# Row statistics taken chunk by chunk, later rotation tables on GpSimd, column statistics by pairs, zero fill behind the loads: one change to a fused decoder kernel

## The chip, the cores and the metric

The kernel runs on one core of a Trainium2 chip. The metric is device time in microseconds for one execution of the whole program; the median of three runs before the change is 1200.24 us (1200.2 to 1203.42). The profile is of one further execution.

## The reference, cut to what matters

Input `x` has 8 sequences of 256 rows and 1024 features, so 2048 rows. Three branches are added to it one after the other, each on a layer norm (without weights) of what came before.

```python
x = x + attn(_layernorm(x), ...)            # 4-layer decoder, width 128, on the sequences
x = x + xattn(_layernorm(x), ctx_4096, ...) # channel mask from the context, gates, conv, batch norm
x = x + ffn(_layernorm(x), gate_w, expert_w)# 8 experts of 1024x1024, two for each row

# attn: h = LN(x) @ Win.T + bin, then four times:
y = silu(layernorm(h, l1w, l1b))
y = sconv(y, phazor, last_conv)  # causal convolution with p**t, p = tanh|phz| * exp(i*angle)
h = h + y * scl
y = silu(layernorm(h, l2w, l2b) @ w1.T + b1) @ w2.T + b2
h = h + y
# and: layernorm(h) @ Wout.T + bout
# xattn: for each (sequence, feature) column the top 154 of 256 rows of ctx are "kept":
_, topk_idx = jax.lax.top_k(cm, k)
mask = zeros.at[b_idx, l_idx, topk_idx].set(1.0)
kept, dropped = mask * LN(x), (1 - mask) * LN(x)  # max and mean of both give two gates
```

## The kernel before, in words

**Tiling.** Features lie on the 128 partitions. The 2048 rows are four chunks of 512 (two sequences each); `xs[c]` holds chunk c as 128 partitions x 8 feature groups x 512. All arithmetic is fp32.

**Row statistics.** The projection needs mean and standard deviation of each row of `x`. For these, `x` is loaded a second time with rows on the partitions: `load_rows(c)` (L380) brings 2 MB into a tile of the pool `maskp` (tag `mask`, one buffer, the later home of the mask), takes `bn_stats` of 4 x 2 stretches of 512 on VectorE (L387), `bn_aggr` (L388), and a power of -1/2 on GpSimd (L393). L396 to L407 issue the loads on SyncE's queue: rows and x of chunk 0, the first quarter of the context, `w1`, `w2`, then rows and x of chunks 1, 2, 3 with a second quarter of the context between. Behind them L408 to L413 queue a zero fill of 9 MB (18 DMAs of 512 KB) into the output and one block of a scratch tensor.

**Tables.** Layer l's convolution is written as: multiply by cos and sin of the phase, a real scan with `decay`, multiply again. The table `turn` (4 layers x cos and sin x 256) is doubled in eight steps by angle addition in `phases(some)` (L426): for layer 0 alone four VectorE instructions a step (L439 to L442), for layers 1 to 3 together six (L446 to L451). L453 starts a block of high priority, in which the powers of the phase, the table of layer 0 (L495), `decay`, the initial values and `turned_w` are traced. After it come the centring of `win` (L517 to L530), `start(0)`, two steps of search, and the folding of `w1`, `w2`, `b1`, `b2` (L548 to L565).

**Cells.** Each of 16 cells (layer, chunk) goes through `recurrence` (L583: `inverse_std` of h, y, silu, table, four scans L594, table L597), `second_norm` (L600) and `feedforward` (L614). `inverse_std` (L568) is a chain over four engines: square on ScalarE, eight small matmuls L574, `ve` on VectorE L351, the power on GpSimd L352, four broadcasting transposes L166. `start(c)` (L532) projects chunk c into h[c]. The loop L687 runs recurrence of cell n, then second_norm of n-1, feedforward of n-2, and for the last layer `put_out` and `normed_x1` of n-3 and `kept_and_dropped` of n-4 (L306: for each column of the chunk kept and dropped values, their max on VectorE L315 and sums on ScalarE L318). The tables of layers 1 to 3 are traced at n = 0 (L691), `weights_out` (load and folding of `wout`) at n = 4.

**Search.** Beside this a threshold search over the context finds the mask. Each of four quarters (16 columns by 128 partitions) is a generator (`search`, L204): a guess from `bn_stats` of each column (L216), four trials of 16 ScalarE activations that count (L233), a finish on VectorE (three instructions a column, L255 to L258), and the mask (L281). `advance(n)` (L289) traces n of these sections; two searches can be under way, the second from the third step on. Context tiles have tag `ctx` and two buffers. One detail of L216 matters: `bn_stats` gives count, mean and squared deviation of the even-numbered elements in fields 0 to 2 and of the odd ones in 3 to 5, and the guess reads fields 1 and 2 alone.

**Order.** The code is traced once. A scheduler then orders each engine's instructions, by the order of tracing as priority and by when its own model of times says an input is ready; every engine then runs its list strictly in that order. A tile with one buffer can be loaded again only when its last reader is done.

**Afterwards** come the gates and convolution, the routing, and a long stage in which TensorE multiplies rows by expert weights.

Of the kernel before, what the change touches and what calls it, by code (L numbers as in the profile page):

```python
# [9 lines left out]
F32 = mybir.dt.float32  # L10
U8 = mybir.dt.uint8
# [5 lines left out]
P = 128  # L17
# [50 lines left out]
def decoder_kernel(ctx: ExitStack, tc: tile.TileContext, x_t, x_rows, ctx_t, vecs, win_t, w1_t, w2_t, wout_t,  # L68
# [106 lines left out]
    with ExitStack() as early:  # L175
# [28 lines left out]
        def search(hb):  # L204
# [10 lines left out]
            for i in range(GH):  # L215
                v.bn_stats(st[:, i, :], ctx_h[:, i, :])  # L216

            sd = small("sd")
            v.tensor_scalar(sd, st[:, :, 2], 2.0 / S, TINY, ALU.mult, ALU.add)
# [4 lines left out]
            v.scalar_tensor_tensor(trial[:, 0], sd, -SHARE, st[:, :, 1], ALU.mult, ALU.subtract)  # L224
# [64 lines left out]
        def advance(n):  # L289
            nonlocal steps  # L290
            for _ in range(n):
                if waiting and (not going or (len(going) == 1 and steps >= 3)):
                    going.append(waiting.pop(0))
# [34 lines left out]
        with ExitStack() as dec:  # L328
# [50 lines left out]
            rows = []  # L379
            def load_rows(c):  # L380
                r = maskp.tile([P, CT // P, D], F32, tag="mask", name="rows")
                nc.sync.dma_start(out=r, in_=x_rows[c])
                mv = lp.tile([P, 4, 2], F32, tag="mv", name="mv")
# [13 lines left out]
            load_x(0)  # L397
            ctxs.append(load_ctx(0))
            nc.sync.dma_start(out=w1, in_=w1_t)
            nc.sync.dma_start(out=w2, in_=w2_t)  # L400
            load_rows(1)
            load_x(1)
            load_rows(2)
            load_x(2)
            ctxs.append(load_ctx(1))
            load_rows(3)
            load_x(3)  # L407

            zero = tkp.tile([P, S], F32, tag="hid", name="zero")
            nc.gpsimd.memset(zero, 0.0)  # L410
            for rows_ in [x2_rows[0:P, :]] + [out[i * P : (i + 1) * P, :] for i in range(NT + 1)]:
                nc.sync.dma_start(out=rows_.rearrange("p (a w) -> p a w", w=S),
                                  in_=zero.unsqueeze(1).to_broadcast([P, D // S, S]))  # L413


            mask = maskp.tile([P, B, NK, S], U8, tag="mask", name="mask")


            v = nc.vector
# [5 lines left out]

            def phases(some):  # L426

                one = some.stop - some.start == 1
                cos, sin = turn[:, some, 0, :], turn[:, some, 1, :]
                v.memset(cos[:, :, 0:1], 1.0)  # L430
                v.memset(sin[:, :, 0:1], 0.0)
                for m, (pc, ps) in enumerate(powers):
                    n = 1 << m
                    lo, hi = slice(0, n), slice(n, 2 * n)
                    tmp = lp.tile([P, 2, 2, S], F32, tag="mi", name="tab_tmp")
                    tmp = tmp.rearrange("p a b t -> p (a b) t")[:, 0 : some.stop - some.start, lo]
# [16 lines left out]
            with tc.high_priority():  # L453
# [57 lines left out]
                for l in range(DEPTH):  # L511
                    v.tensor_scalar(turned_w[:, l], center, col("sc_lin", l), None, ALU.mult)
# [768 lines left out]
```

## Time and profile before

| what | value |
|---|---|
| median of three runs | 1200.24 us |
| profiled execution | 1200.54 us, span 1198.8 us |
| TensorE busy (matmul records) | 1000.2 us, 83% of the span |
| VectorE busy | 580.4 us, 48% |
| ScalarE busy | 476.4 us, 40% |
| GpSimd busy | 261.9 us, 22% |
| mean granted TensorE clock | 0.90 |
| DMA | 144.99 MB, mean 121 GB/s |

How to read it: shares over the whole span hide that stages have different limits, so the stages are read one by one. In the rows of the timeline the first number is the start in us from the start of the span, the second the duration in us, then engine, line, operation and tiles, and in brackets the idle time of the engine before it with what ended it. In the rows by stage each engine has busy us and, in brackets, its number of instructions; then come the granted clock, the DMA share and GB/s.

### The profile page before, as it was taken

To read this page: it belongs to the slowest core of one execution; us is meant where nothing else is said; L and a number is where in the kernel's file an instruction comes from. 1 tells how busy PE (TensorE), PEld (TensorE's weight loads), DVE (VectorE), ACT (ScalarE), POOL (GpSimd) and SP (SyncE) were. 2 spreads that over 40 slices of the span, in tenths; PEclk is the share of its full clock that TensorE was granted. 3 is DMA by queue.
4 is the path that set the end of the run, shared out by engine and by line. 5 is a ranking of instruction groups with operands and counts; after the bars stand their busy time and mean duration, and the time that the engine had idled before them with its cause. 6 is when DMAs were issued, how large, how long until landed. Compare 5 with 4: busy or idle time off the path is not lost. (4 is left out here: it accounts for less than half of the span.)

```text
span 1198.8 us, 10179 instructions
## 1 busy us (share of the span) xinstructions
PE 1000.2 (83%) x2954; PEld 493.5 (41%) x2954; DVE 580.4 (48%) x1779; ACT 476.4 (40%) x1167; POOL 261.9 (22%) x275
## 2 busy tenths in 40 slices
PE   4848878878888666268649999999999999999994
PEld 2524434434444333134324444444444444444442
DVE  7588888868958988687635111111111111111110
ACT  0577667676773566595211121111111111111110
POOL 1111111121111000104367321112313214131111
PEclk9768889889989877577669999999999999999998
DMA  9495010000000000035534956463648567583622
GB/s 386 190 384 165 0 71 1 36 36 1 1 1 1 0 1 1 12 141 194 158 107 127 329 149 169 110 171 84 197 113 240 138 193 213 133 247 91 175 35 37
DMA packets 53840, 144.99 MB, mean 121 GB/s; under 512 B 5232, under 2 KB 14448, under 8 KB 51984
## 3 DMA queue, kind: packets, MB, share of 16 engines
q0 software_dynamic: 17728, 59.88, 20.3%
q1 hardware_dynamic: 35472, 83.97, 19.9%
q8 instruction: 25, 0.41, 0.1%
q10 hardware_dynamic: 576, 0.41, 0.1%
q14 instruction: 39, 0.32, 0.1%
HBM read 106.61 MB, written 37.64 MB: 120 GB/s over the span
## 5 line engine op out<-in xcount | busy, mean ns | idle before, releaser
L1091 PE MATMUL ps_mm<-w_x,xT 128*128 128x512 f32 x1152 | 505.4, 597 | 3.2 <-ACT xT L1085 1.0
L1091 PEld LDWEIGHTS ps_mm<-w_x,xT 128*128 128x128 f32 x1152 | 216.4, 190 | 270.8 <-issue 258.9
L1094 DVE SCALAR_TENSOR_TENSOR y<-ps_mm,held,y 128x512 f32<-128x512 f32 x56 | 42.0, 751 | 358.9 <-PE ps_mm L1091 358.9
L233 ACT ACTIVATE tkj<-ctx,tk_trial 128x256 f32<-128x256 f32 x256 | 129.1, 504 | 40.1 <-DVE tk_trial L248 22.7
L1077 ACT ACTIVATE y<-src,held 128x1024 f32<-128x1024 f32 x28 | 32.1, 1147 | 188.2 <-DMA out_dram<-y,to 155.1
L1085 ACT COPY xT<-ps_tp 128x512 f32<-128x512 f32 x37 | 21.6, 585 | 193.6 <-PE ps_tp L1083 181.4
L352 POOL TENSOR_TENSOR rs<-ve,minus_half 128x4 f32<-128x4 f32 x36 | 41.1, 1141 | 246.7 <-DVE ve L351 224.2
L618 PE MATMUL ps_tp<-z,w 128*128 128x512 f32 x128 | 70.6, 658 | 13.8 <-DVE z L611 12.9
L1095 POOL DMA_INDIRECT out_dram<-y,to x28 | 44.4, 1586 | 162.5 <-DVE y L1094 120.6
L166 PE MATMUL ps_st<-ident,rs 128*128 128x128 f32 x160 | 30.0, 323 | 56.3 <-POOL rs L352 48.0
L1064 POOL DMA_INDIRECT src<-x_rows,to x28 | 29.0, 1036 | 162.0 <-ACT y L1077 160.8
L318 ACT ACTIVATE comb<-comb 128x256 f32<-128x256 f32 x128 | 51.5, 403 | 27.2 <-DVE smax L315 25.5
L624 PE MATMUL ps_mm<-f,w 128*128 128x512 f32 x128 | 62.0, 604 | 0.0
L1094 DVE SCALAR_TENSOR_TENSOR y<-ps_mm,got,y 128x512 f32<-128x512 f32 x18 | 13.5, 750 | 99.8 <-PE ps_mm L1091 93.1
L166 PEld LDWEIGHTS ps_st<-ident,rs 128*128 128x128 f32 x160 | 20.8, 161 | 82.0 <-POOL rs L352 71.9
L621 ACT ACTIVATE f<-ps_tp,b1f 128x512 f32<-128x512 f32 x64 | 43.5, 681 | 24.2 <-PE ps_tp L618 23.8
L1083 PE MATMUL ps_tp<-ident,xn 128*128 128x128 f32 x296 | 39.9, 278 | 13.9 <-ACT xn L1075 13.9
L1083 PEld LDWEIGHTS ps_tp<-ident,xn 128*128 128x128 f32 x296 | 35.4, 144 | 33.4 <-issue 19.0
L574 PEld LDWEIGHTS ps_cols<-mean_w,sq 128*128 128x128 f32 x288 | 38.9, 199 | 23.2 <-ACT sq L571 11.6
L233 ACT ACTIVATION_READ_ACCUMULATOR tkj<-ctx,tk_trial 128x1 f32 x256 | 48.3, 189 | 0.0
L604 PE MATMUL ps_mm<-mi,turned_w 128*128 128x512 f32 x64 | 38.2, 704 | 7.9 <-DVE mi L597 7.8
L964 POOL DMA_INDIRECT meta<-pay,at x32 | 36.0, 1124 | 39.3 <-DVE ts_mv L889 18.9
(370 smaller groups left out, 1441.8 us busy)
## 6 DMA issues: line engine op xcount, KB each, us to landing
w_x<-in_expert_w_dram SPq DMA_DIRECT2D x36, 1024.0 KB, 7.5
out_dram<-zero SPq DMA_DIRECT2D x17, 512.0 KB, 7.3
rows<-in_x_rows_dram SPq DMA_DIRECT2D x4, 2048.0 KB, 8.3
x<-in_x_t_dram SPq DMA_DIRECT2D x8, 1024.0 KB, 11.5
ctx<-in_ctx_t_dram SPq DMA_DIRECT2D x16, 512.0 KB, 8.3
x_rows<-row SPq DMA_DIRECT2D x16, 512.0 KB, 4.9
w<-in_w_t_dram SPq DMA_DIRECT2D x2, 1024.0 KB, 10.6
win<-in_win_t_dram SPq DMA_DIRECT2D x1, 512.0 KB, 3.9
```

The costliest lines, as they stand in the source:

```text
L166: nc.tensor.transpose(rb[:, q * P : (q + 1) * P], rs[:, q : q + 1].to_broadcast([P, P]), ident)
L233: nc.scalar.activation(junk, ctx_h[:, i, :], AF.Sign, bias=trial[:, 0, i : i + 1], accum_out=trial[:, 1, i : i + 1])
L318: nc.scalar.activation(comb[:, st, :], comb[:, st, :], AF.Copy, accum_out=ssum[:, st, b, k : k + 1])
L352: nc.gpsimd.tensor_tensor(out_, ve, root, ALU.pow)
L574: nc.tensor.matmul(out=st[:, q : q + 1], lhsT=sq[:, q * P : (q + 1) * P], rhs=mean_w, start=True, stop=True)
L618: nc.tensor.matmul(out=fps, lhsT=w1[:, l, f * P : (f + 1) * P], rhs=z, start=True, stop=True)
L621: nc.scalar.activation(ft, fps, AF.Silu, bias=b1[:, 4 * l + f : 4 * l + f + 1])
L624: nc.tensor.matmul(out=xc, lhsT=w2[:, l, f, :], rhs=ft, start=False, stop=(f == DFF // P - 1), skip_group_check=True)
L1083: nc.tensor.transpose(tp[:, k * P : (k + 1) * P], xn[:, kk * P : (kk + 1) * P], ident)
L1091: nc.tensor.matmul(out=op, lhsT=xT[:, k * P : (k + 1) * P], rhs=ws[k][g], start=(k == 0), stop=(k == NK - 1))
L1094: nc.vector.scalar_tensor_tensor(y[:, o], op, weight, y[:, o], ALU.mult, ALU.add)
L1095: added = nc.gpsimd.indirect_dma_start(out=out[0:ROWS_THEN, :] if apart else out, out_offset=bass.IndirectOffsetOnAxis(ap=token, axis=0), ...
```

## The change

Four things are edited, and a few that go with them.

1. `load_rows` only loads; the statistics are a function of their own, `rows_std(c)`. Chunk 0's is traced behind the loads, that of chunk n+1 in the loop, ahead of `start(n+1)`. Row tiles of odd chunks use a buffer of tag `ctx` instead of `mask`. The loads are in a new order: rows and x of chunks 0 and 1, context quarter 0, `w1`, `w2`, x of 2 and 3, rows of 2; rows of 3 are loaded at n = 0 and context quarter 1 at n = 2.
2. `phases` becomes a generator that runs on VectorE for layer 0 and on GpSimd for layers 1 to 3; of the latter, three doubling steps are traced at each of n = 1, 2, 3, the first instruction of each step behind `y` of the current cell (`begun`). Its temporary is of tag `sq`.
3. The search's guess takes one `bn_stats` for two columns: it reads 128 even-numbered elements of each, interleaved, so that fields 0 to 2 are those of the first column and 3 to 5 those of the second.
4. The zero fill is traced at n = 4, behind `y` of cell 4 and the load of `wout`; its source is a tile of tag `sq` of 1024 elements.

Beside these: the centring of `win` moves ahead of the tables, the table of layer 0 and `turned_w` leave the high-priority block, the folding of `w1` and `w2` moves to n = 1, that of `wout` to n = 8. `advance` gets one step at n = 0 and 1 (three before), and a second search starts from the fourth step.

```diff
-            for i in range(GH):
-                v.bn_stats(st[:, i, :], ctx_h[:, i, :])
+            for i in range(0, GH, 2):
+                v.bn_stats(st[:, i : i + 2, :].rearrange("p c f -> p (c f)")[:, 0:6],
+                           ctx_h[:, i : i + 2, ::2].rearrange("p c s -> p s c"))
...
-                if waiting and (not going or (len(going) == 1 and steps >= 3)):
+                if waiting and (not going or (len(going) == 1 and steps >= 4)):
...
             def load_rows(c):
-                r = maskp.tile([P, CT // P, D], F32, tag="mask", name="rows")
+                if c % 2:
+                    r = tkp.tile([P, CT // P, D], F32, tag="ctx", name="rows", bufs=2)
+                else:
+                    r = maskp.tile([P, CT // P, D], F32, tag="mask", name="rows")
                 nc.sync.dma_start(out=r, in_=x_rows[c])
+                loaded.append(r)
+
+            def rows_std(c):
+                r = loaded[c]
                 mv = lp.tile([P, 4, 2], F32, tag="mv", name="mv")
...
             load_rows(0)
             load_x(0)
+            load_rows(1)
+            load_x(1)
             ctxs.append(load_ctx(0))
             nc.sync.dma_start(out=w1, in_=w1_t)
             nc.sync.dma_start(out=w2, in_=w2_t)
-            load_rows(1)
-            load_x(1)
+            load_x(2)
+            load_x(3)
+            rows_std(0)
             load_rows(2)
-            load_x(2)
-            ctxs.append(load_ctx(1))
-            load_rows(3)
-            load_x(3)
...
                 one = some.stop - some.start == 1
+                v = nc.vector if one else nc.gpsimd
...
+                    behind = list(begun)
-                    v.tensor_tensor(cos[:, :, hi], cos[:, :, lo], cb, ALU.mult)
+                    after(v.tensor_tensor(cos[:, :, hi], cos[:, :, lo], cb, ALU.mult).ins, behind, "in turn")
...
+            start(0)
+            advance(2)
+            table = phases(slice(1, DEPTH))
             for n in range(len(cells) + 4):
                 if n < len(cells):
                     scanned[n] = recurrence(*cells[n])
-                if n == 0:
-                    phases(slice(1, DEPTH))
                 if n + 1 < NCH:
+                    rows_std(n + 1)
                     start(n + 1)
+                    if n == 0:
+                        load_rows(3)
+                    if n == 1:
+                        weights_in()
+                    if n == 2:
+                        ctxs.append(load_ctx(1))
+                    if n == 1:
+                        mask = maskp.tile([P, B, NK, S], U8, tag="mask", name="mask")
+                if 0 < n < NCH:
+                    for _ in itertools.islice(table, 3):
+                        pass
                 if n == NCH:
-                    wo, wo_mean, bo_mean = weights_out()
+                    wo = load_wo()
+                    zeroes()
+                if n == NCH + 4:
+                    wo_mean, bo_mean = weights_out(wo)
...
-                advance(3)
+                advance(1 if n < 2 else 3)
```

`weights_in()` holds the folding of `w1` and `w2` as it was; `zeroes()` holds the zero fill.

## The prediction

> **What bounds the kernel now.** The page's chain of work that ended last only says that TensorE ends the run (it covers 1% of the span), so I read the busy times by stage first. Columns: TensorE, weight load, VectorE (DVE), ScalarE (ACT), GpSimd (POOL), clock, DMA.
>
> ```profile
> 0.00:41.00 41.00, 20.28 (x67) 14.52 (x67) 29.31 (x150) 8.95 (x25) 7.93 (x36) 0.92 0.86 347
> 41.00:82.00 41.00, 25.23 (x57) 12.81 (x57) 29.66 (x101) 25.37 (x82) 7.16 (x5) 0.71 0.74 280
> 82.00:410.00 328.00, 274.79 (x905) 139.96 (x904) 269.49 (x811) 223.20 (x614) 46.58 (x41) 0.91 0.11 38
> 410.00:490.00 80.00, 45.34 (x138) 24.37 (x138) 66.49 (x259) 54.33 (x227) 5.89 (x13) 0.71 0.00 1
> 490.00:640.00 150.00, 94.12 (x339) 50.31 (x340) 103.15 (x340) 63.64 (x114) 54.87 (x65) 0.69 0.40 123
> 640.00:1198.80 558.80, 540.44 (x1453) 251.50 (x1451) 82.26 (x120) 100.95 (x106) 139.46 (x115) 0.99 0.58 158
> ```
>
> From 640 us on TensorE is busy at clock 0.99 with expert rows: the change doesn't touch that, nor 490 to 640 (gates, routing). What the change can move is the stretch to 490. There no engine is full; VectorE is the fullest: 336.0 of the 408 us from 82 to 490, that is 82%, with 72 us idle. TensorE has 84% of 82 to 410 but only 57% after that. Before 82 VectorE is busy 59.0 of 82. So I look at the order of its work there (timeline of VectorE):
>
> ```profile
> 52.87 0.17 DVE L248 TENSOR_TENSOR tk_trial<-tk_ends,tk_w 128x16 f32<-128x16 f32 x1
> 59.39 1.88 DVE L387 BATCH_NORM_STATS2 bn<-rows 128x6 f32<-128x512 f32 x3 [6.34 <-DMA rows<-in_x_rows_dram]
> ...
> 72.40 1.88 DVE L387 BATCH_NORM_STATS2 bn<-rows 128x6 f32<-128x512 f32 x3 [1.49 <-DMA rows<-in_x_rows_dram]
> ...
> 77.94 0.16 DVE L351 TENSOR_SCALAR ve<-ps_cols 128x4 f32<-128x4 f32 x1
> ...
> 81.30 0.69 DVE L586 TENSOR_TENSOR y<-h,ps_st 128x512 f32<-128x512 f32 x1 [1.80 <-PE ps_st L166]
> ```
>
> and what TensorE (its timeline) and the load queue do:
>
> ```profile
> 44.08 1.71 PE L574 MATMUL ps_cols<-mean_w,sq 128*128 128x1 f32 x8
> 45.65 13.44 PE L536 MATMUL ps_tp<-x,win 128*128 128x512 f32 x24
> ```
> ```profile
> 51.04 0.33 SPq L382 DMA_DIRECT2D rows<-in_x_rows_dram  x1
> ```
> ```profile
> 64.48 0.33 SPq L382 DMA_DIRECT2D rows<-in_x_rows_dram  x1
> ```
>
> The first cell's variance (L574) is done at 45.8, but VectorE takes it up (L351) at 77.94, because the statistics of rows 1, 2 and 3 stand ahead of it in its list, and rows 2 and 3 can each be loaded (51.04, 64.48) only after the one buffer was read. The first cell's `mi` (L591) starts at 82.9, some 40 us later than its inputs would allow, and VectorE idles 23 us before 82.
>
> **The parts, with their cost.** *Statistics by chunk, loads, weight folding.* Nothing is removed: eight `bn_stats` and what goes with them took 45.96 to 51.57, so 5.6 us a chunk. What moves is their place: behind cell n's recurrence. Then cell 0 depends on win, x0, rows 0. h[0] came out of VectorE (L541) at 34.0, after waiting for a GpSimd power that ended at 33.65 (2.8 us of idle), and TensorE then ran the folding of `w1` (L561, 35.4 to 42.4) ahead of L574; that folding now sits at n = 1. From h at 33: bias and square on ScalarE 1.3, L574 1.1 to 1.7, `ve` 0.2, power 1.0, L166 1.1 to 2.0, y 0.7, table load and silu 1.3 + 0.8: `mi` at about 41 instead of 82.9. By then VectorE has done what it did by 41 before (29.3), less the reduction of `w2` (L549, 2.3) and half of one quarter's `bn_stats` (2.7), plus rows_std(1), whose rows now have their own buffer (5.6): 30. The new order on SyncE's queue (rows 2 behind rows_std(0), then rows 3, context 1) costs nothing while the data come before use: the 14 MB moved in the first 41 us (347 GB/s) cover win, rows and x 0 and 1, context 0, `w1`, `w2`, part of x2. x3 and rows 2 end near 50, rows_std(2) is due near 60. Without that cover it costs what it did: 6.3 us a chunk.
>
> *Tables on GpSimd.* VectorE loses L446 to L451: six lines of 2.0 to 2.07 us, 12.1 us. GpSimd gets 48 `tensor_tensor` with 4590 elements in all. The nearest row is its `tensor_tensor` L754, 129 elements in 0.525 us; its 8-element cast takes 0.18, so I take 0.17 us + 2.75 ns an element: 8.2 + 12.6 = 21 us, in blocks of 3.4, 5.8 and 11.6 us at n = 1, 2, 3. Behind them in GpSimd's list wait the powers of `inverse_std`, and behind these TensorE's L166. In the cell stage two powers lie 6 to 8 us apart, so only the third block overhangs, by some 4 us. I charge 3 us; bounds 0 (VectorE and TensorE have other cells' work) and 10 (every block delays one power by half).
>
> A rule speaks against this part. VectorE and GpSimd meet in this trace:
>
> ```profile
> 259.60 1.23 DVE L597 TENSOR_TENSOR mi<-mi,turn 128x1024 f32<-128x1024 f32 x1
> ```
> ```profile
> 259.78 1.91 POOL L352 TENSOR_TENSOR rs<-ve,minus_half 128x4 f32<-128x4 f32 x1 [6.92 <-DVE ve L351]
> ```
> ```profile
> 493.89 0.52 POOL L754 TENSOR_TENSOR vacant<-vacant,past 128x129 f32<-128x129 f32 x1
> 493.92 0.58 DVE L806 TENSOR_SCALAR zc<-row,vec 128x128 f32<-128x128 f32 x1
> ```
>
> The power takes 1.01 us alone and 1.91 when it comes behind L597. The other way round, VectorE's L808 has a median of 0.352 and took 0.506 beside an L754: 0.15 us on a GpSimd instruction of 0.53, or 30%. The Trainium skill (SBUF — State Buffer, Who interferes with whom) says more: a VectorE instruction with two SBUF inputs and a GpSimd one that reads SBUF block each other for a whole instruction. Scans, L591, L597 and L257 are of that kind, 100 of the 253 us from 82 to 335, 40%. By the row: 21 x 0.4 x 0.3 = 2.5, I take 3 us. By the rule: nearly the remaining GpSimd time whenever one of them is next, 21 x 0.4 to 0.5, or 8 to 10 us; then the move gives back most of its 12.1. I keep 10 as the bound.
>
> *Column statistics by pairs.* 64 instructions at a pitch of 0.336 us become 32 of as many elements: 10.8 us less, half before 82 and half in the cells. The new read jumps to another column at every element. The skill (the same page, Specifications) wants two hits per 16-byte line for full rate; at half rate one takes near 0.6, and only 2.3 us are saved. The nearest row: L224 reads 16 elements 24 bytes apart in 0.179 us, its neighbours L225 and L226 without that 0.175 and 0.168. No row here strides wider, so I take the nearest, 10.8, and keep 2.3.
>
> *Zero fill, `wout`, `advance`.* The fill occupied SyncE from 65.9 to 97.6; nothing on VectorE waited for it, and behind it stands a context load that waits for its buffer to 163.9. At n = 4 (near 120 to 150) it stands ahead of the same load: 0. If the buffer is free earlier, that load is up to 30 us late, which search's slack takes. The folding of `wout` moves within the cells: 0.
>
> **Sum.** VectorE to 490: 395.0 - 12.1 - 10.8 + 3 = 375. Of this 30 is done by 41; 345 remain. I keep the share of 82 to 490 (0.8235), since the same chains and orders make its idle time: 419, end at 460 instead of 490. With 3 us for the table's blocks: 27 us less, 1200.54 - 27 = 1173.5 in the profiled execution. That ran 0.3 us above the median of 1200.24: 1173.
>
> **Rivals.**
> - *Cells keep their pace* (16.7 us from L591 to L591), so the whole advance of 41 us survives: 1159. For: VectorE's load shrinks. Against: cells 0 to 3 now hold the statistics.
> - *The costs go to their bounds*: stride at half rate, blocking 10: 390.5 - 32 = 358.5, / 0.8235 = 435, end 476, with 8 us of table delays 484: 1194.
> - *The change doesn't do what it says*: the planner still puts statistics of rows 2 and 3 ahead of the first `ve`, because its model lets rows land early. Then `mi` waits for rows 3 (near 60) and some 12 us of idle remain: 1185.
> - *Slower: the search becomes the end.* Context 1 takes the rows' buffer, so it is loaded after rows_std(3) (near 87), lands near 97, and its first trial ends near 125 instead of 114.9. Eleven more trials at the old 22.5 us give 372, the last mask 51 us later, 423 (412.8 before). `kept_and_dropped` of chunk 3 began at 474.8, now 447: slack 24. It decides once trials are over 2.2 us longer; at 28 us (ScalarE shared with denser cells) the end is 36 us beyond the slack: 1173 + 36 = 1209. Against: ScalarE is only 68% busy there.
>
> **Chances and range.** Main 0.58 (own range 1162 to 1184), pace kept 0.13, bounds 0.12, planner 0.09, search 0.08. The range 1157 to 1193 leaves out the search, and parts of the pace and bounds cases. 0.3% (3.6 us) is about what a measurement tells from no change: faster 0.89, within 0.03, slower 0.08.
>
> **What would show it.** Right: first L591 near 41; no wait of L387 for rows over 2 us; L446 to L451 on GpSimd at about 21 us; 32 L216 at 0.34; the last L315 near 460; 490 to 1199 shifted as a block. Wrong: L216 near 0.6; scans and L597 stretched beside GpSimd; the cell stage's VectorE share below 0.8; L315 of chunk 3 waiting for the mask.

## The result, and the profile after

The changed kernel takes 1211.91 us (median of four runs, 1210.1 to 1213.42), the kernel before on the same chip 1201.22: a ratio of 1.0086, 95% interval 1.0064 to 1.0107. It is 0.9% slower; 1173 was forecast. The profiled execution of the changed kernel took 1213.42 us, span 1211.7, against 1200.54 and 1198.8.

Four events cut the stretch that the change touches: the first `mi` (L610, L591 before), the fifth, the sixteenth and last, and the end of the column sums of `kept_and_dropped` (L321, L315 before). Each is taken at the start of the instruction, the last one for a group. First the changed kernel by these stages, with the rest as the last row; columns as in the prediction's first view.

```profile
0.00:40.60 40.60, 21.60 (x65) 12.24 (x66) 32.22 (x147) 5.52 (x7) 8.04 (x39) 0.87 0.96 394
40.60:133.60 93.00, 70.14 (x223) 38.66 (x223) 55.18 (x123) 51.73 (x151) 40.98 (x59) 0.80 0.21 83
133.60:309.70 176.10, 152.88 (x534) 79.67 (x533) 139.84 (x406) 126.46 (x347) 33.12 (x28) 0.95 0.21 81
309.70:499.60 189.90, 119.65 (x347) 59.88 (x345) 153.63 (x563) 120.42 (x437) 12.07 (x19) 0.77 0.00 1
499.60:1211.70 712.10, 634.93 (x1790) 301.51 (x1790) 185.53 (x461) 166.03 (x228) 195.14 (x180) 0.92 0.54 150
```

and the kernel before:

```profile
0.00:82.90 82.90, 45.63 (x122) 27.34 (x122) 59.00 (x252) 35.20 (x108) 15.09 (x41) 0.81 0.80 315
82.90:148.30 65.40, 54.07 (x185) 29.43 (x186) 56.15 (x174) 48.75 (x139) 7.53 (x9) 0.87 0.35 117
148.30:333.60 185.30, 154.73 (x511) 77.95 (x511) 152.02 (x457) 131.15 (x362) 31.86 (x26) 0.91 0.06 23
333.60:487.40 153.80, 111.20 (x349) 56.95 (x347) 127.33 (x438) 95.01 (x333) 13.08 (x19) 0.84 0.00 1
```

The rest is a block: 712.1 us against 711.4. So all of the loss is in the end of the sums, 499.6 instead of 487.4. The first `mi` did come 42.3 us earlier. At the fifth 14.7 of these are left, at the sixteenth 23.9, and at the end it is 12.2 us late. The numbers to read are VectorE's (the third engine of each row): up to the fifth `mi` it did 87.4 us of work instead of 115.2, and after it 293.5 instead of 279.4, although it has 13.6 us less to do in all (380.9 against 394.5). So behind the fifth `mi` there are 14 us more work and 13 us more idle time (72.5 against 59.7), and these are more than the 14.7 us that it came earlier. The loss itself lies behind the last `mi`: from there to the end it is 189.9 us instead of 153.8, and most of the difference stands ahead of the last cell's output `h` (101.4 us to it instead of 72.0, with 74.1 us of VectorE work instead of 56.9). TensorE's work is no larger: 364.3 us up to the end, 365.6 before.

Where the first cells lost their lead stands in the timelines of the changed kernel, first TensorE's, then VectorE's, and behind them VectorE's row for the same `z` in the kernel before. (ScalarE had squared cell 0's sum, for the cell's second norm, in a row of 0.60 us from 56.95.)

```profile
57.88 8.68 PE L556 MATMUL ps_tp<-x,win 128*128 128x512 f32 x16
66.40 3.63 PE L580 MATMUL ps_cols<-vec,w 128*128 128x1 f32 x32
69.89 1.10 PE L556 MATMUL ps_tp<-x,win 128*128 128x512 f32 x2
70.83 1.16 PE L593 MATMUL ps_cols<-mean_w,sq 128*128 128x1 f32 x8
```
```profile
40.56 1.23 DVE L610 TENSOR_TENSOR mi<-y,turn 128x1024 f32<-128x1024 f32 x1
...
71.99 1.88 DVE L401 BATCH_NORM_STATS2 bn<-rows 128x6 f32<-128x512 f32 x3
...
81.51 0.17 DVE L242 TENSOR_SCALAR tk_is_low<-tk_trial 128x16 uint8<-128x16 f32 x1 [6.98 <-ACT tkj L239]
...
85.24 0.16 DVE L357 TENSOR_SCALAR ve<-ps_cols 128x4 f32<-128x4 f32 x1
...
89.22 0.69 DVE L630 TENSOR_TENSOR z<-ps_mm,rbs 128x512 f32<-128x512 f32 x1 [0.29 <-ACT rbs L628]
```
```profile
105.68 0.66 DVE L611 TENSOR_TENSOR z<-ps_mm,rbs 128x512 f32<-128x512 f32 x1
```

Squared at 57.55, cell 0's mean starts on TensorE at 70.83, behind the projection of chunk 2 and the folding of `w1`; done at 72.0, VectorE takes it up (L357) at 85.24, behind the statistics of chunk 2 and a 7 us wait of the search for ScalarE. That is 13.3 and 13.2 us. It is the fault that the prediction saw at cell 0's first norm, moved on to its second: `mi` to `z` (L630) takes 48.7 us instead of 22.8, so 26 of the 42 us are gone, and the cell's output `h` stands at 112.1 instead of 120.8.

The search is the other part. The second quarter's columns share buffers with the odd chunks' rows, and go out at 92.46 (SyncE's queue); the columns are in use from 100 us on, and its guess (L229), one search step a cell behind the first quarter's four trials, stands at 142.7 (79.0 before). Its first trial ends at 166.5 instead of 114.9.

```profile
92.46 1.75 SPq L198 DMA_DIRECT2D ctx<-in_ctx_t_dram  x4
```

The last trial ends at 423.3 instead of 361.9, the last mask at 476.5 instead of 412.5. So two quarters' finishes, not one, lie behind the last `mi`. VectorE's groups from 309.7 to 499.6 of the changed kernel, and from 333.6 to 487.4 of the one before:

```profile
L321 DVE CUSTOM_DVE_ANT_0 comb<-x,mask 128x256 f32<-128x256 f32 x64 | 26.6, 419 | 8.1 <-ACT comb L324 8.0
...
L261 DVE TENSOR_SCALAR_CACHE_REDUCE hid<-ctx,tk_t 128x256 f32<-128x256 f32 x32 | 15.2, 475 | 0.1
```
```profile
L315 DVE CUSTOM_DVE_ANT_0 comb<-x,mask 128x256 f32<-128x256 f32 x64 | 26.2, 419 | 2.1 <-ACT comb L318 2.0
...
L255 DVE TENSOR_SCALAR_CACHE_REDUCE hid<-ctx,tk_t 128x256 f32<-128x256 f32 x16 | 7.6, 474 | 0.1
```

32 of the search's passes stand there instead of 16, and the sums wait 8.0 us instead of 2.0 for ScalarE, which now has trials to run beside them; all 8.0 lie ahead of the last `h`.

### The profile page after: what moved, and what is told of

Read it like the earlier page. It is cut to its first block, busy times and chain, and to the rows that moved or that the text cites. A ratio compares the mean times of both kernels' runs of the same rounds, so it can differ in the third digit from the quotient of the medians.

```text
span 1211.7 us, 10123 instructions
## 1 busy us (share of the span) xinstructions
PE 999.2 (82%) x2954; PEld 492.0 (41%) x2954; DVE 566.4 (47%) x1697; ACT 470.2 (39%) x1167; POOL 289.3 (24%) x325
## 5 line engine op out<-in xcount | busy, mean ns | idle before, releaser
L643 PE MATMUL ps_mm<-f,w 128*128 128x512 f32 x128 | 65.2, 629 | 9.5 <-ACT f L640 9.5
L640 ACT ACTIVATE f<-ps_tp,b1f 128x512 f32<-128x512 f32 x64 | 43.3, 680 | 14.7 <-PE ps_tp L637 14.4
L239 ACT ACTIVATION_READ_ACCUMULATOR tkj<-ctx,tk_trial 128x1 f32 x256 | 48.5, 189 | 0.0
```

The lines of the kernel that those rows point to most:

```text
L239: nc.scalar.activation(junk, ctx_h[:, i, :], AF.Sign, bias=trial[:, 0, i : i + 1], accum_out=trial[:, 1, i : i + 1])
L640: nc.scalar.activation(ft, fps, AF.Silu, bias=b1[:, 4 * l + f : 4 * l + f + 1])
L643: nc.tensor.matmul(out=xc, lhsT=w2[:, l, f, :], rhs=ft, start=False, stop=(f == DFF // P - 1), skip_group_check=True)
```

## The experiments

All on one core; names that begin with a are edits of the changed kernel, with b of the kernel before. Times are medians, ratios are to the kernel before on the same chip with their 95% interval; the events are from each one's profiled execution (us), as is VectorE's busy time up to the end of the sums. Executions of one kernel lie up to 9.5 us apart, and the profiled one up to 5 us off the median (a_three_undone 1209.55, a_ctx_first 1206.36), so a few us in the events mean nothing by themselves. The letters in the text (S, T, L and so on) are those by which the forecasts name their theories.

| kernel | time | ratio | first mi | fifth mi | last mi | last h | last mask | end of sums | VectorE busy |
|---|---|---|---|---|---|---|---|---|---|
| before | 1201.2 to 1204.2 | 1 | 82.9 | 148.3 | 333.6 | 405.6 | 412.5 | 487.4 | 394.5 |
| changed | 1211.9 | 1.0086 [1.0064, 1.0107] | 40.6 | 133.6 | 309.7 | 411.1 | 476.5 | 499.6 | 380.8 |
| a_two_trials | 1200.1 | 0.9988 [0.9979, 0.9996] | 40.3 | 140.7 | 337.9 | 412.3 | 331.8 | 485.7 | 373.0 |
| b_two_trials | 1211.3 | 1.0065 [1.0042, 1.0089] | 88.0 | 146.2 | 349.2 | 423.0 | 335.8 | 496.2 | 386.0 |
| a_search_first | 1230.8 | 1.0234 [1.0210, 1.0258] | 40.3 | 130.1 | 312.1 | 426.0 | 489.0 | 516.9 | 381.7 |
| a_tables_dve | 1207.1 | 1.0047 [1.0028, 1.0066] | 40.2 | 131.0 | 320.9 | 405.9 | 451.9 | 492.5 | 386.2 |
| a_stats_ahead | 1215.3 | 1.0097 [1.0070, 1.0124] | 40.5 | 146.9 | 328.5 | 411.7 | 458.1 | 502.9 | 381.2 |
| a_ctx_first | 1210.0 | 1.0055 [1.0039, 1.0072] | 48.5 | 138.0 | 313.9 | 404.0 | 455.0 | 491.7 | 381.8 |
| a_only_stats | 1205.3 | 1.0035 [1.0016, 1.0054] | 41.9 | 127.6 | 313.6 | 405.3 | 451.3 | 489.4 | 395.5 |
| b_paired | 1207.0 | 1.0027 [1.0011, 1.0043] | 86.5 | 152.2 | 327.1 | 404.9 | 425.4 | 495.1 | 385.7 |
| b_search_sched | 1214.8 | 1.0107 [1.0081, 1.0133] | 82.3 | 143.4 | 335.5 | 412.1 | 434.9 | 500.4 | 392.5 |
| b_tables_pool | 1212.0 | 1.0097 [1.0077, 1.0116] | 84.7 | 141.3 | 340.7 | 418.7 | 420.1 | 498.5 | 389.0 |
| a_three_undone | 1214.3 | 1.0106 [1.0086, 1.0125] | 48.4 | 145.7 | 330.8 | 407.4 | 438.7 | 494.3 | 391.4 |
| a_wi_early | 1212.8 | 1.0100 [1.0080, 1.0120] | 52.1 | 130.0 | 318.6 | 414.4 | 458.7 | 496.8 | 379.7 |
| a_early_search | 1213.6 | 1.0094 [1.0076, 1.0111] | 42.9 | 147.2 | 334.1 | 412.7 | 428.4 | 499.7 | 381.4 |
| a_early_search_v | 1223.9 | 1.0173 [1.0151, 1.0195] | 46.0 | 157.5 | 352.0 | 427.5 | 431.9 | 508.7 | 396.1 |
| b_zero_last | 1207.0 | 1.0038 [1.0021, 1.0056] | 83.4 | 148.2 | 338.0 | 413.4 | 417.9 | 494.5 | 394.5 |
| b_wo_late | 1210.6 | 1.0072 [1.0055, 1.0090] | 83.0 | 148.3 | 341.4 | 415.7 | 411.7 | 495.5 | 395.2 |
| b_one_norm | see text | | 81.5 | 131.9 | 283.9 | 353.5 | 401.0 | 445.7 | 385.8 |
| a_one_norm | see text | | 40.3 | 128.0 | 282.2 | 351.6 | 435.6 | 458.2 | 375.1 |

The first theory was that the late search sets the end by itself; the rivals were GpSimd's tables, and the list of VectorE's work being laid differently.

**Half of the trials, in both kernels** (two of four trials of each quarter are left out, and the search's flag of failure is put to zero).

```diff
-TRIALS = 5
+TRIALS = 3
...
         v.tensor_reduce(bad, fails, AX.X, ALU.max)
+        v.tensor_scalar(bad, bad, 0.0, None, ALU.mult)
```

> The changed kernel with two trials a search instead of four, and the flag that calls the slow path put to zero: it leaves out half of the threshold search, so the mask is only near the right one. Theory S (the search is the end: 16 trials in a row at 22 to 29 us each in the company of the cells, last mask at 476.5 us): eight trials less take some 180 us from the chain, the last mask comes before 330, the end of the first part falls from 503 to what VectorE's work allows, and the run to about 1165 us. Theory T (tables on GpSimd stretch VectorE and hold up the powers in the cells): the search is only filler, its trials are ScalarE time that nobody waits for; about 1205 us.

> The kernel before with the same cut of the search (two trials of four, flag at zero; half of the search left out). Theory S: there the last mask (412.5) has 62 us of slack to its reader (474.8), so the cut saves only VectorE time, some 10 us: about 1190 us, and the changed kernel with the same cut is 20 us or more below it. Theory T: the same 5 to 10 us as in the changed kernel, which then stays 10 us behind: about 1193 us.

The masks are ready at 332 in the one and 336 in the other, far ahead of need. The changed kernel gains 12 us by it and no more; the kernel before, with some 67 us of ScalarE work and 8.5 of VectorE work taken away, becomes 8 us slower. Both theories had the kernel before at 1190 to 1193, so neither forecast came. The search as the only cause falls, and so does ScalarE's load as a bound of the kernel before; the same cut moves the two kernels to opposite sides.

**The first quarter's search ahead of the others** (three steps from the first cell on, the second quarter only after eight steps).

```diff
-                if waiting and (not going or (len(going) == 1 and steps >= 4)):
+                if waiting and (not going or (len(going) == 1 and steps >= 8)):
...
-                    if n == 2:
-                        ctxs.append(load_ctx(1))
...
-                advance(1 if n < 2 else 3)
+                advance(3)
```

> The changed kernel with three search steps at n = 0 and 1 too, the second search only after the first (its context is loaded by itself, the load at n = 2 goes). Theory S: the first quarter's four trials are traced ahead of cell 1 and run at 14 to 16 us, so they end near 110 instead of 142.6, the last mask moves from 476 to about 450, and the run falls by 15 to 25 us, to about 1190 us. Theory T: no change beyond 4 us, about 1211 us.

It delays the second quarter further: last mask 489, end 516.9. S and T had forecast 1190 and 1211, and both missed. With later masks the end came later here; this says nothing on earlier ones.

**The tables back on VectorE.**

```diff
-                v = nc.vector if one else nc.gpsimd
+                v = nc.vector
```

> The changed kernel with the tables of layers 1 to 3 on VectorE (the move to GpSimd undone alone). Theory S: VectorE has 118 us idle before 490, so the 12 us come back into gaps; the trials wait as before: 1208 to 1216 us. Theory T: scans and table products lose their 3.3 us of stretching, and the powers no longer queue behind blocks of up to 12 us: 1200 us or less.

4.8 us come back, and VectorE's busy time grows by 5.4 only, not by the 12.1 of the tables: 3.3 of the difference are scans and rotations that GpSimd's steps had stretched, the rest was not taken apart. Tables on GpSimd cost this kernel about 5 us; the time lies between the ranges of S and T. One wait is in the changed kernel's trace: a variance is ready at 105.2, and its power begins at 108.22, behind the table steps.

**Statistics of the rows one cell earlier, and the first quarter's columns ahead of the second chunk's rows.**

```diff
             table = phases(slice(1, DEPTH))
+            rows_std(1)
...
-                    rows_std(n + 1)
+                    if n + 2 < NCH:
+                        rows_std(n + 2)
```
```diff
+            ctxs.append(load_ctx(0))
             load_rows(1)
             load_x(1)
-            ctxs.append(load_ctx(0))
```

> The changed kernel with each chunk's row statistics one cell earlier (chunk 1 ahead of the loop, chunk n+2 at n). Theory R (the statistics at their projection hold up the next cells: rows 2 stand on VectorE from 72 to 84 behind the wait of the search's is_low, so the third mi comes at 100.7, 40 us after the second): the third mi moves to about 85, and VectorE's idle time between the first and the fifth mi falls from 38 to about 25; the run to about 1202 us. Theory F (what is missing in this stage is other work for VectorE, since the first search finish comes at 143 instead of 115): the third mi moves, but the fifth stays within 6 us of 133.6, and the run within 5 us of 1212.

> The changed kernel with the first context quarter loaded ahead of rows and x of chunk 1, as before the change. Theory F: the first trial starts near 36 instead of 46.9, the first search's four trials end some 10 us earlier than 142.6, its finish fills VectorE earlier, and the last mask comes 10 us before 476; the run falls to about 1203 us. Theory R: rows and x of chunk 1 land 5 us later, nothing else changes: within 4 us of 1212.

The first puts more work between cell 0's `mi` and its `z` (56.8 us) and the fifth `mi` falls back to 146.9; the third, which R put at 85, comes at 104.7 (100.7 in the changed kernel), so R fails, and F has only the time right. The second delays the first `mi` by 8 us and still brings the last mask 21 us forward, where F said 10; the end is no later than the changed kernel's, and the time lies in R's range.

**The changed kernel without tables on GpSimd and without pairs; and pairs alone in the kernel before.**

```diff
-            for i in range(0, GH, 2):
-                v.bn_stats(st[:, i : i + 2, :].rearrange("p c f -> p (c f)")[:, 0:6],
-                           ctx_h[:, i : i + 2, ::2].rearrange("p c s -> p s c"))
-            st = st.rearrange("p (h c) f -> p h (c f)", c=2)[:, :, 0:6].rearrange("p h (c f) -> p h c f", c=2)
+            for i in range(GH):
+                v.bn_stats(st[:, i, :], ctx_h[:, i, :])
+            st = st.rearrange("p (h c) f -> p h c f", c=2)
```

> The changed kernel with two parts undone: tables of layers 1 to 3 on VectorE, one bn_stats a column. What is left is the statistics by chunk with the new load order, the tracing order and the late zero fill. Tables on VectorE alone gave 1207 us. If pairing gains what it saves on VectorE (8.7 us at a pitch of 0.40 instead of 0.336), this run is at about 1214 us, and the statistics part alone is what makes the kernel slower than before. If VectorE has room (118 us idle), pairing is worth nothing and this run is at 1207 us.

> The kernel before with the column statistics by pairs as the one edit: 32 bn_stats of 0.40 us pitch instead of 64 of 0.336, 8.7 us of VectorE time less, half of it before 82 us where VectorE waits for rows, half in the cells. If VectorE's time is what counts (the prediction's model): 1196 us. If the order in which the lists interleave decides, anything from 1194 to 1206 us.

Taking the pairs away adds 9.3 us of VectorE work and costs no time (1207.1 to 1205.3). Putting them into the kernel before takes away 8.8 and makes it 0.27% slower. So VectorE's load does not by itself set the end.

**Search schedule alone, tables on GpSimd alone, in the kernel before; three parts undone together, and the folding of the weights ahead of the loop, in the changed one.**

```diff
-                if waiting and (not going or (len(going) == 1 and steps >= 3)):
+                if waiting and (not going or (len(going) == 1 and steps >= 4)):
...
-                advance(3)
+                advance(1 if n < 2 else 3)
```
```diff
                 one = some.stop - some.start == 1
+                v = nc.vector if one else nc.gpsimd
...
-                    tmp = lp.tile([P, 2, 2, S], F32, tag="mi", name="tab_tmp")
-                    tmp = tmp.rearrange("p a b t -> p (a b) t")[:, 0 : some.stop - some.start, lo]
+                    tmp = lp.tile([P, 2, CT], F32, tag="sq", name="tab_tmp").rearrange("p a t -> p (a t)")
+                    tmp = tmp[:, 0 : (some.stop - some.start) * n].rearrange("p (l t) -> p l t", t=n)
```
```diff
             advance(2)
+            weights_in()
             table = phases(slice(1, DEPTH))
...
-                    if n == 1:
-                        weights_in()
```

> The kernel before with one part of the change: the search's schedule (one step instead of three after each of the first two cells, and the second quarter may join after four steps instead of three). VectorE's work is the same as before, nothing else is moved. Theory L (the later search carries its VectorE finish and its ScalarE trials into the output cells): last mask at 430 or later instead of 412, end of the column sums near 495 instead of 487, time 1206 to 1211. Rival H (the loss of the changed kernel sits in its first four cells, where the small search steps stand ahead of the cells' work; the schedule itself costs nothing): the first four cells of this kernel are no slower than before, end near 487, time 1198 to 1203.

> The kernel before with one part of the change: the tables of layers 1 to 3 on GpSimd, at the place where VectorE made them. VectorE has 12.4 us less to do. Theory T (GpSimd's steps stretch the scans beside them, and what VectorE gains turns into idle time): end of the column sums 487 to 493, time 1201 to 1208. Rival G (VectorE bounds this stretch, and work taken off it is gained): end near 480, time 1190 to 1195.

> The changed kernel with three of its parts undone: tables back on VectorE, column statistics one column at a time, the first quarter's columns loaded ahead of the second chunk's rows. Rows' statistics by chunk, the search's schedule, the order of the preparation and the zero fill stay as changed. If the effects measured one by one add up (4.8, 1.8 and 1.9 us less than the changed kernel), 1203.4, ratio 1.002. If each only shuffles a list of fixed order, they don't add up: 1205 or more. If the late first quarter was what kept the search late, the last mask stands before 440 and the time is below 1199.

> The changed kernel with the feedforward weights prepared ahead of the loop over the cells, as in the kernel before, instead of after the second cell. Theory W (the 40 us between the second and the third rotation come from that preparation, put between two cells, and its wait for TensorE): first rotation near 50 instead of 40.6, the gap before the third near 25, the fifth rotation at 128 or earlier, end near 494, time 1205 to 1208. Rival (the gap is set by the third chunk's own statistics and by the search's steps ahead of them in the list): the gap stays over 35, time 1209 to 1216.

The schedule alone costs 1.07%: the cells are as before up to the last `mi` (335.5 against 333.6), then the masks come 22 us late and the sums 13. That is the course that L forecast, though the time is above its 1206 to 1211; H falls. The tables alone cost 0.97%, with another course: the fifth `mi` comes 7 us earlier, as G would have it, but the last one 7 us later, and the time is above the ranges of both G and T. The parts don't add up: with the tables, pairs and columns undone together the kernel is slower (1.0106) than with the first two alone (1.0035). With the weights folded early, the third `mi` follows the second by 26.2 us instead of 40.6, as W said; the way from the first `mi` to the first `z` shrinks to 29.9 us, and cell 0's output comes at 102.1 instead of 112.1. But the fifth `mi` gains only 3.6 us by it, the last `h` stands at 414.4 and the time is no better (1.0100). So the long wait at the second norm is real, and yet not all that holds the first cells.

**The changed kernel with the early search, whole and without tables and pairs; and two moves in the kernel before that touch little.** In the first two all rows pass through the mask's buffer, so both quarters of columns are loaded early (the mask's tile is made behind the last rows, and each chunk's rows are loaded behind the statistics of the chunk before):

```diff
-                if c % 2:
-                    r = tkp.tile([P, CT // P, D], F32, tag="ctx", name="rows", bufs=2)
-                else:
-                    r = maskp.tile([P, CT // P, D], F32, tag="mask", name="rows")
+                r = maskp.tile([P, CT // P, D], F32, tag="mask", name="rows")
...
             load_x(2)
+            ctxs.append(load_ctx(1))
             load_x(3)
...
-                advance(1 if n < 2 else 3)
+                advance(3)
```
```diff
                 if n == NCH:
+                    zeroes()
                     wo, wo_mean, bo_mean = weights_out()
```
```diff
-                if n == NCH:
+                if n == NCH + 4:
                     wo, wo_mean, bo_mean = weights_out()
```

> The changed kernel with the search back where it was: all rows pass through the mask's buffer one chunk after the other, so both quarters of columns are loaded early, and the schedule is the old one (three steps after each cell, the second quarter after three steps). Tables on GpSimd, pairs, statistics by chunk and the late zero fill stay. Theory L (the late search eats the head start): first trial of the second quarter near 115 to 130 instead of 166, last mask before 430 instead of 476, end of the column sums 475 to 485, time 1187 to 1197, faster than before. Rival O (any order of the list ends near 490 to 500): masks earlier, but the end at 490 to 500, time 1202 to 1212.

> The same, with the tables on VectorE and the column statistics one column at a time, so that of the change only the statistics by chunk, the order of the preparation and the late zero fill are left. Theory L: last mask before 430, end 472 to 482, time 1184 to 1194. Rival O: end 490 to 500, time 1202 to 1212.

> The kernel before with the zero fill behind the fourth cell instead of ahead of the loop, all else as it was. No work of VectorE, ScalarE or TensorE is touched. If only queues and work count, 1199 to 1203 (ratio within 0.003 of 1). If any edit lays the list differently (rival O), the ratio is outside that, 1.004 or more.

> The kernel before with the output weights prepared after the eighth cell instead of the fourth, as the changed kernel does; the same instructions, some 60 us later, still 140 us ahead of their first use. If only work and waits count, 1199 to 1203. If any edit lays the list differently (rival O), the ratio is outside 0.997 to 1.003.

L falls as the whole cause: the second quarter's first trial ends at 140.2, the last mask moves from 476.5 to 428.4, and the end stays at 499.7, because the fifth `mi` falls back from 133.6 to 147.2, with 75.2 us of VectorE work between the first and the fifth instead of 55.2. The early time was given either to the cells or to the search. The second of the two (1223.9) lies outside both forecasts: with 14.7 us more VectorE work than the first it ends 9 us later, while a_only_stats, with as much work, ends at 489.4.

Over the 16 kernels with both norms and all trials, the stretch from the last `mi` to the last `h` grows with the last mask: 72 to 79 us where the mask is there by 439, 83 to 96 where it comes from 451 to 459, 101 and 114 where it comes at 476 and 489. So a late search does fill that stretch. The end doesn't follow (487 to 509, 489 to 503, 500 and 517), for where the search is late the cells ahead of it can run earlier.

The two small moves cost time without adding work. The zero fill behind the fourth cell costs 0.38%, a little under the 1.004 that O asked for; the same instructions of the output weights, some 70 us later and over 100 us before their use, cost 0.72%, as O forecast. Both kernels are level with the one before at the fifth `mi` (148.2 and 148.3). VectorE runs 1320 instructions up to the end of the sums; the longest sequences that the two traces have in common with the kernel before hold 1080 and 1086 of them (matched by kind and by number within the kind), so one moved piece lays nearly a fifth of the list anew. Neither is a pure change of order: the fill has another source tile and its transfers now run beside the cells, and the output weights take 9.5 us of TensorE's and 5.6 of VectorE's time from a place where they delayed nothing into the midst of the cells. All six edits of the kernel before that keep both norms made it slower, by 0.27 to 1.07%, three of them with less VectorE work, so the 1.07% of b_search_sched is not for certain the price of a late search.

**Without the second norm of each cell, in both kernels** (that norm is left out, so the values that are routed differ, and the rest of the run takes 832 us instead of 712; only the end of the sums is compared).

```diff
-                rb = inverse_std(xc)
-                rbs = line_tile("rbs")
-                nc.scalar.copy(rbs, rb)
                 z = lp.tile([P, CT], F32, tag="z", name="z")
-                nc.vector.tensor_tensor(z, xc, rbs, ALU.mult)
+                nc.vector.tensor_scalar(z, xc, 1.0, None, ALU.mult)
```

> The kernel before, with part of the computation left out: the second normalisation of each cell (its square on ScalarE, its mean and its transposes on TensorE, its power on GpSimd, its copy) is gone and VectorE passes the sum on as it is. VectorE loses about 2.5 us of work, ScalarE some 19, GpSimd some 24; what goes is above all a wait of every cell. Theory C (the chain from engine to engine sets the pace of the cells): pitch of the cells from 16.8 to 14 or less, last output of the cells before 370, end of the column sums 445 to 460. Rival V (VectorE's load sets it): end 480 to 486.

> The changed kernel with the same norm left out. Theory C, with the head start kept once the chain is short: end 10 to 25 us ahead of that of the kernel before cut in the same way. Theory O (the head start is lost to the order of the lists whatever the chain): end within 10 us of it, or behind it. Rival V: end 485 to 497.

The whole times are 1283.3 (1.0674 [1.0641, 1.0707]) and 1292.3 (1.0727 [1.0704, 1.0750]). The stages of b_one_norm, then of a_one_norm:

```profile
0.00:81.50 81.50, 44.11 (x122) 25.77 (x122) 59.00 (x252) 35.17 (x108) 15.09 (x41) 0.77 0.81 318
81.50:131.90 50.40, 43.48 (x147) 22.01 (x148) 44.71 (x130) 40.62 (x117) 4.49 (x6) 0.94 0.45 154
131.90:283.90 152.00, 129.76 (x381) 61.29 (x382) 141.02 (x408) 111.36 (x303) 20.84 (x15) 0.96 0.08 28
283.90:445.70 161.80, 109.21 (x324) 54.83 (x322) 141.02 (x515) 106.83 (x381) 10.04 (x17) 0.80 0.00 1
```
```profile
40.30:128.00 87.70, 65.00 (x186) 33.51 (x185) 53.79 (x121) 49.83 (x147) 36.89 (x56) 0.76 0.23 89
128.00:282.20 154.20, 135.96 (x408) 65.72 (x407) 137.32 (x386) 110.56 (x309) 19.01 (x17) 0.95 0.24 92
282.20:458.20 176.00, 108.81 (x317) 55.10 (x315) 151.80 (x570) 123.05 (x447) 11.24 (x18) 0.77 0.00 1
```

The end comes 41.7 us earlier in the one and 41.4 in the other, with 8.7 and 5.7 us of VectorE work less: the rest is idle time of VectorE that is gone. From the fifth to the last `mi` the pitch of the cells falls from 16.8 to 13.8 and from 16.0 to 14.0, and VectorE is now busy 93% and 89% there (82% and 79% with the norm). So the norm, and not VectorE's work, had held the cells: V falls, and C's forecast for the kernel before came in all three numbers. But the cut takes more than a wait. TensorE's work up to the end falls from 365.6 to 326.6 us and from 364.3 to 331.4, that is 39 and 33 us, and its share from the fifth to the last `mi` stays near 85% (84 before, 87 changed, 85 and 88 here). Whether the chain of waits or TensorE's part of the norm set the pace is not shown.

For the changed kernel C had hoped to keep the head start once the norm is gone, and that fails; O's forecast came. The head start is lost as before, in the same stage (87.7 us for four cells, VectorE at 61%), for here too its list holds cell 0 from 40.3 to a `z` at 85.1. The last outputs `h` then come together (351.6 and 353.5), and the changed kernel ends 12.5 us behind, all of it behind the last `h`, where its search still runs (last mask 435.6 against 401.0). In the whole kernels the same split is 5.5 us at the last `h` and 6.7 behind it.

## Why the prediction was wrong, step by step

- *The first `mi` near 41* was right: 40.6, and no `bn_stats` of rows waits for a load there. The reading behind it, a variance that waits in VectorE's list, was right too, but it was applied to one place. The change puts `rows_std(2)`, `start(2)` and the weights' folding ahead of `second_norm(0)`, and the same kind of wait came back at that norm, 13.3 us for TensorE and 13.2 for VectorE. The clause that failed is "behind cell n's recurrence. Then cell 0 depends on win, x0, rows 0": that holds for its first norm only.
- *Work of VectorE*: 375 forecast, 380.8 measured; 345 left at 41 forecast, 348.6 measured. This is 4.4 us of end at the forecast share, a small part. (The forecast counts to 490, 2.6 us behind the last sum of the kernel before.) The pairs saved 8.8 to 9.3 instead of 10.8, and the tables' beside work gave back 3.3 us in scans and rotations where 3 was said.
- *"I keep the share of 82 to 490 (0.8235), since the same chains and orders make its idle time"* is the step that failed. From 40.6 to the end it was 348.6 / 459.0 = 0.76. At 0.8235 the three stages would have taken 26.0, 6.3 and 3.3 us less, in the order of time; with 4.4 more for the work and 0.4 less for the earlier first `mi`, this is the 39.6 us between 460 and 499.6. Two things were wrong in it. The orders were not the same: the first four cells ran at 0.59. And the share was no property of VectorE: without the second norm it was 93%, so what VectorE waited for had set it, and work taken from VectorE can turn into idle time there. Over the 16 kernels with both norms and all trials VectorE's busy time runs from 380 to 396 us and the end from 487 to 517, and the least work does not go with the earliest end; TensorE's lies between 363 and 376 us and does not order the ends either.
- *Tables on GpSimd, 3 us of chain*: in the changed kernel they cost 4.8 us net; alone in the kernel before 0.97%. The sum had them as a gain of (12.1 - 3) / 0.8235 - 3, that is 8 us.
- *Zero fill and `wout`: 0*. By themselves 0.38% and 0.72% in the kernel before. What changed in both is the order of VectorE's list and the place of some work or transfers, and the prediction had no price for that.
- *The slower rival, "the search becomes the end"*, put the second quarter's first trial at 125 and the last mask at 423. They came at 166.5 and 476.5. The columns were there when it said; what it left out is the edited `advance`, which holds the guess back to 142.7. Its point of decision, trials over 2.2 us longer, was not reached: the eleven trials lie 23.3 us apart, not 22.5. So 1209 came near the measured time in part by luck: the mechanism is half of it. The last mask did come late, but giving the search its place back doesn't mend the end (a_early_search).

What is shown: the wait at cell 0's second norm (trace); that the search's schedule alone, with no work added, makes the end 13 us later in the kernel before (b_search_sched); that less work on VectorE (b_paired, b_tables_pool) or ScalarE (b_two_trials) does not by itself bring the end forward; and that the second norm holds the cells (the pair without it). Not shown is by what the norm holds them, its chain of waits or its work on TensorE, whose work and clock were not varied by themselves. That a list with `second_norm(0)` ahead of chunk 2's statistics would keep the lead was not tried. Why just these moved pieces cost 5 to 13 us stays open: which pairs of instructions in the new order matter was not taken apart. No version that does the whole work and beats the kernel before came out of these runs; the one ratio below 1 (a_two_trials, 0.9988) leaves half of the search out.

## What to carry to other kernels

A busy share of 82% on the fullest engine is not yet a bound: before work on that engine is turned into time, ask what its idle 18% waits for. Here one norm left out for each cell brought the end 41 us forward with under 9 us of that engine's work, so look at such a step, and at all engines that it uses, ahead of the fullest engine's work. When a step is moved out of a critical wait, follow the same item to its next wait in the same lists, and write down every instruction that now stands ahead of it there. And where a planner lays the lists, measure a move that should cost nothing first: here two of those cost 4.6 to 8.7 us, which is the size of the effects that one would like to read.

## What the runs showed of the hardware

Scans beside GpSimd's table steps, in the changed kernel (VectorE, then GpSimd):

```profile
123.25 2.46 DVE L613 TENSOR_TENSOR_SCAN mi<-decay,init_a,mi 128x256 f32<-128x256 f32 x2
125.63 2.58 DVE L613 TENSOR_TENSOR_SCAN mi<-decay,init_b,mi 128x256 f32<-128x256 f32 x2
```
```profile
121.72 0.82 POOL L482 TENSOR_TENSOR turn<-turn,pc 128x384 f32<-128x384 f32 x1
...
123.17 0.83 POOL L483 TENSOR_TENSOR tab_tmp<-turn,ps 128x384 f32<-128x384 f32 x1
123.95 1.21 POOL L485 TENSOR_TENSOR turn<-turn,pc 128x384 f32<-128x384 f32 x1
125.12 1.38 POOL L484 TENSOR_TENSOR turn<-turn,tab_tmp 128x384 f32<-128x384 f32 x1
```

Two scans take 2.46 and 2.58 us here, and 1.39 without GpSimd beside them (at 61.33), so a scan loses 0.5 to 0.6 us, where the prediction's row (0.15 us on a GpSimd step of 0.53) gave less. A table step of one shape (L482, L485) took 0.82 us at 121.72, with VectorE idle, and 1.21 beside the scans. The steps took 26.1 us on GpSimd, not the estimated 21. In all VectorE's scans and rotations grew by 3.3 us for the 12.1 moved, near the lower of the prediction's two figures (3 and 10).

The strided statistics by pairs (one instruction's durations in ns: least, median, most), changed and before:

```profile
L217 DVE BATCH_NORM_STATS2 tk_st<-ctx x32: 395/474/489, 35.2 to 294.6; 128x6 f32<-128x256 f32 x32
```
```profile
L216 DVE BATCH_NORM_STATS2 tk_st<-ctx x64: 367/409/428, 22.9 to 246.8; 128x6 f32<-128x256 f32 x64
```

The jump to another column at every element adds 0.065 us to 0.41, where the prediction's worse case had near 0.6 in all.
